# Last image's routing split seven blocks and one, and expert weights held in nine places and reloaded by halves

## Chip, core and metric

The kernel runs on one core of a Trainium2 chip. The metric is device time in microseconds (us) from launch to the last instruction, median of several executions. All arithmetic is fp32. The engines have separate in-order instruction streams: TensorE (PE, with PEld for its weight loads), VectorE (DVE), ScalarE (ACT), GpSimd (POOL) and SyncE (SP). In this kernel SP issues nearly all DMAs, ACT a few stores, POOL the gathers. A queue waits at its head: an instruction that waits holds back all behind it on that engine.

## The reference

Four images of 128 channels x 4096 positions pass through two layers, each adding to its input: a convolutional attention (softmax over 4096 x 4096 scores), and then a token layer that does a second attention and an expert feed-forward. The feed-forward is what the change is about:

```
logits = x @ gate_w.T + gate_b           # 4096 tokens x 64 experts, x layer-normalised
probs = softmax(logits, axis=1)          # over the tokens of the image
topv, topi = top 8 tokens of each expert
pooled[e] = sum_k topv[k,e] * x[topi[k,e]]
out[e] = gelu(pooled[e] @ weight1[e] + b1[e]) @ weight2[e] + b2[e]     # 128 -> 512 -> 128
y[topi[k,e]] += topv[k,e] * out[e]
```

So each image needs, per expert, its eight best tokens, the softmax sum, and the weighted sum of those tokens; one matrix product pair per expert; and a spread of the results over the tokens, done as a product with a matrix M that holds the probabilities of the chosen tokens and zeros elsewhere.

## The kernel before

The work is a series of stages, `stage(b, layer, ...)`, one per image `b` and attention layer; the last is `stage(3, 1)`. Each runs eight query blocks `n` of 512 tokens, and each block eight steps `g` of four key tiles. At every step one piece of the other work is emitted: `step_after` advances what follows a finished block (`finish_attn`), `beside` prepares the next stage. A fence that costs no instruction (`tc.no_sync_barrier`) keeps emitted work in its step; within the fences a planner orders each engine's instructions by when it computes that they are ready. `tc.keep_in_program_order` forbids it to move one instruction ahead.

`finish_attn` for block `n` combines the products (L626-636), divides and adds the residual (L645-654), normalises the tokens (`norm_tokens`, with the power on POOL, L181), stores them in DRAM in `tokens` (L614) for the later gather, turns them to channel order, and computes the gate logits into `M` (L696-701) and each block's eight largest per expert into `cand` (L704). Blocks other than the last of image 3 are turned with a DVE transpose and DMAs through DRAM (L321, L333, L683); the last one with PE transposes and ACT copies (`to_channels`, L356-357).

Routing of images 0 to 2 lies beside a later stage (`route`). Image 3 has none to lie beside. After its last block, `early_sums` takes exponential sums of seven blocks (L826) and `last_route` does the rest: `places` finds the eight places (maximum L729, index search over 4096 columns L731), `gather` fetches four token rows per partition by indirect DMA on POOL (L740), `replace` (L747) writes a copy of M without the eight best, `weigh` (L766-768) and a product with `twin` (L775) give the pooled vectors in `pooledT` (L776), and exponentials (L866) with DVE subtractions (L867) turn M into the spread matrix, whose discarded copy `z` is in a 2 MB buffer.

The experts go in 16 groups of four. A group's weights (first and second matrix, two halves of 1 MB) are one 2 MB load from a packed copy in DRAM (L947). Groups 0 and 1 are loaded during `stage(3, 1)`, 2 to 7 after it into buffers that attention leaves, group 8 into `z`, and 9 to 15 through a ring of four. Per group: `first_product` (L1013) and its copy (L1018), `hidden` (four PE transposes L1023, bias L1027, Gelu on ACT L1031), `second_product` (L1043). The loop emits the first product of group g, the hidden step of g-1 and the second product of g-2. After the loop come a range check (`watch`, from L1578), transposes of the results to expert order (L1061-1062), a reload of the first two images' M (2 MB, L1069) and of the inputs `x2` (eight of 1 MB, L1079), and per image pair eight products with M (L1092), each added by DVE (L1099); every two blocks are stored by two DMAs of 0.5 MB (L1102).

## Time and profile before

| what | value |
|---|---|
| median of 3 runs | 3320.46 us (3320.09 to 3320.47) |
| profiled execution: its own time / span of instructions | 3322.09 / 3320.4 us |
| PE busy | 3226.2 us, 97% |
| DVE, ACT, POOL busy | 2119.4, 1250.7, 413.3 us |
| last attention product ends | 3174.98 us from the span's start |
| first expert product starts | 3214.31 us |
| last expert product of the loop ends | about 3280.3 us |
| DMA, mean over the span | 68 GB/s |

Times in the views are us from the start of the span unless they are durations. In a timeline row come start, duration, engine, line, operation, tiles written and read, and the number of instructions joined in the row. The table by stage gives for each engine busy time and instruction count, then the clock that PE was granted as a share of full speed, the mean busy share of the 16 DMA engines and their rate.

### The profile page before, as it was taken

The page shows a single profiled execution, that of the slowest core. Times are in us where ns is not written, and L with a number is a line of the kernel's source. Part 1 is how long each engine was busy: PE and PEld are TensorE (multiplying, and loading weights), DVE is VectorE, ACT ScalarE, POOL GpSimd, SP SyncE. Part 2 cuts the span into 40 slices and gives each one's busy share as a digit, 9 for nine tenths or more (in the row PEclk, how much of TensorE's full clock was granted, in tenths as well). Part 3 has the DMA queues.
Part 4 walks back from the last instruction along what each step waited for, and adds up shares of the span by engine and source line. Part 5 has one row for each costly group of instructions (what it writes and reads, how often), then busy time and mean ns, then how long its engine had stood idle before and what let it go on. Part 6 is the DMA issues. An engine that isn't in the chain of part 4 may idle for free. (4 is left out here: it accounts for less than half of the span.)

```text
span 3320.4 us, 49374 instructions
## 1 busy us (share of the span) xinstructions
PE 3226.2 (97%) x19744; PEld 1603.4 (48%) x19744; DVE 2119.4 (64%) x4186; ACT 1250.7 (38%) x1429; POOL 413.3 (12%) x410
## 2 busy tenths in 40 slices
PE   8999999999999999999999999999999999999966
PEld 4444444445555544444555554444454454445433
DVE  6665577556675667755766566865775656665654
ACT  3333333333333344333333335333333333443330
POOL 0111113310000004230000003241000002100000
PEclk9999999999999999999999999999999999999977
DMA  3221244223232312301211112311221111021158
GB/s 87 51 54 26 67 107 123 76 77 85 79 85 72 81 32 60 70 23 33 52 42 23 36 36 64 80 42 28 68 51 33 30 30 39 23 80 30 33 227 368
DMA packets 367345, 224.36 MB, mean 68 GB/s; under 512 B 277632, under 2 KB 303232, under 8 KB 363776
## 3 DMA queue, kind: packets, MB, share of 16 engines
q1 hardware_dynamic: 361264, 209.59, 23.3%
q10 hardware_dynamic: 5328, 10.46, 0.8%
q8 instruction: 157, 2.57, 0.3%
q0 software_dynamic: 512, 1.05, 0.1%
q14 instruction: 84, 0.69, 0.1%
HBM read 160.27 MB, written 97.98 MB: 78 GB/s over the span
## 5 line engine op out<-in xcount | busy, mean ns | idle before, releaser
L550 ACT ACTIVATE pt<-ps 128x1024 f32<-128x1024 f32 x1024 | 1021.9, 1025 | 1536.0 <-PE ps L541 1464.3
L541 PE MATMUL ps<-q,t 128*64 128x512 f32 x4096 | 929.7, 593 | 0.0
L475 PE MATMUL av<-pt,asm 64*128 64x512 f32 x4096 | 922.2, 589 | 0.9 <-ACT sw L628 0.9
L565 DVE TENSOR_TENSOR sacc<-sacc,pt 128x1024 f32<-128x1024 f32 x448 | 586.4, 1309 | 291.4 <-ACT pt L550 266.7
L503 PE MATMUL av<-pt,tt 128*64 128x256 f32 x3072 | 637.5, 379 | 0.0
L475 PEld LDWEIGHTS av<-pt,asm 64*128 64x128 f32 x4096 | 395.8, 187 | 485.5 <-issue 470.0
L489 DVE TENSOR_TENSOR tt<-pt 128x512 f32<-128x512 f32 x512 | 356.8, 697 | 380.0 <-ACT pt L550 361.0
L541 PEld LDWEIGHTS ps<-q,t 128*64 128x64 f32 x4096 | 316.3, 137 | 469.7 <-issue 442.8
L503 PE MATMUL av<-tt,mixed 128*64 128x256 f32 x2048 | 526.6, 380 | 5.2 <-DVE tt L489 5.2
L541 PE MATMUL ps<-e,e 64*128 64x512 f32 x2048 | 491.5, 598 | 2.0 <-DMA e<-ye 2.0
L503 PEld LDWEIGHTS av<-pt,tt 128*64 128x64 f32 x3072 | 359.6, 137 | 261.5 <-issue 137.9
L503 PE MATMUL av<-tt,tt 128*64 128x256 f32 x1024 | 305.4, 380 | 0.0
L503 PE MATMUL av<-pt,mixed 128*64 128x256 f32 x1024 | 305.1, 380 | 0.0
L541 PEld LDWEIGHTS ps<-e,e 64*128 64x128 f32 x2048 | 193.3, 187 | 230.2 <-issue 226.2
L503 PEld LDWEIGHTS av<-tt,mixed 128*64 128x64 f32 x2048 | 280.7, 137 | 9.0 <-DVE tt L489 6.5
L181 POOL TENSOR_TENSOR l_y<-l_v,mhalf 128x4 f32<-128x4 f32 x64 | 64.8, 1013 | 1625.4 <-DVE l_v L180 1625.0
L491 DVE TENSOR_TENSOR tt<-pt 128x256 f32<-128x256 f32 x512 | 219.7, 429 | 16.4
L490 DVE TENSOR_TENSOR pt<-tt,pt 128x256 f32<-128x256 f32 x512 | 219.3, 429 | 16.1
L503 PEld LDWEIGHTS av<-pt,mixed 128*64 128x64 f32 x1024 | 140.3, 137 | 61.1 <-DVE pt L490 0.3
L503 PEld LDWEIGHTS av<-tt,tt 128*64 128x64 f32 x1024 | 140.3, 137 | 2.1 <-DVE tt L491 0.8
L584 POOL TENSOR_TENSOR all_sum<-all_sum,c 128x512 f32<-128x512 f32 x32 | 44.0, 1375 | 520.5 <-DVE c L583 520.5
L182 DVE TENSOR_TENSOR l_z<-l_y 128x4 f32<-128x4 f32 x64 | 11.7, 183 | 96.1 <-POOL l_y L181 94.9
(200 smaller groups left out, 1761.0 us busy)
## 6 DMA issues: line engine op xcount, KB each, us to landing
wp<-in_weight_dram SPq DMA_DIRECT2D x128, 256.0 KB
w<-wp SPq DMA_DIRECT2D x16, 2048.0 KB
xq<-in_x_dram SPq DMA_DIRECT2D x32, 256.0 KB
rb<-inv SPq DMA_DIRECT2D x32, 256.0 KB
xT<-xt SPq DMA_DIRECT2D x128, 64.0 KB
ak<-xT SPq DMA_DIRECT2D x32, 256.0 KB
t<-kt SPq DMA_DIRECT2D x128, 64.0 KB
t<-t SPq DMA_DIRECT2D x32, 256.0 KB
```

The source lines that it names most:

```text
L181: nc.gpsimd.tensor_tensor(y[:, :k], v[:, :k], mhalf[:, :k], op=ALU.pow)
L182: nc.vector.tensor_mul(z[:, :k], y[:, :k], y[:, :k])
L475: nc.tensor.matmul(avs[b, 0, n][:, r, :], lhsT=values[b, 0][rows, j, :], rhs=pt[rows, h, :], start=(j == 0), stop=(j == NJ - 1),)
L489: nc.vector.tensor_sub(tt[:, 0:2, :], p4[:, :, 1, :], p4[:, 0, :, :])
L490: nc.vector.tensor_add(p4[:, 0, 1, :], tt[:, 1, :], p4[:, 0, 0, :])
L491: nc.vector.tensor_sub(tt[:, 2, :], p4[:, 1, 0, :], p4[:, 0, 1, :])
L503: nc.tensor.matmul(av[bass.ts(half, HC), bank, slot, :], lhsT=lhsT, rhs=rhs, start=first, stop=final, skip_group_check=True,)
L541: nc.tensor.matmul(ps[part, h, :], lhsT=key[:, part], rhs=q[rows, :], start=True, stop=True,)
L550: nc.scalar.activation(pt, ps, AF.Exp, scale=scale)
L565: nc.vector.tensor_add(sums[b, n], sums[b, n], pt)
L584: nc.gpsimd.tensor_add(all_sum, all_sum, c1)
```

## The change

The last image's routing is split. Block 6 of image 3 is now turned like block 7, by PE. When its logits are there, `early_route`, emitted in the remaining steps of block 7, finds the eight best of the first seven blocks, gathers those rows and takes the exponential sums. After block 7, `last_route` merges these eight candidates with block 7's own eight. Early candidates that drop out get weight zero; the chosen tokens of block 7 are not fetched from DRAM but multiplied: their weights as a 64 x 512 matrix, transposed by PE, times the block's tokens in SBUF. Block 7's tokens are therefore not stored. The replacement over all of M (`last_scores`) comes after the expert loop's step 11 and its exponentials after the loop, with the subtractions on POOL.

The weights have nine places of 2 MB: 0 and 1 are the buffers of the last keys and values, filled by halves in the last block through a hook of `stage`; 2, 6 and 7 are loaded earlier in the stage, 3 to 5 after it, and 8 lies in the space that `finish_attn`'s buffers leave. Groups 9 to 15 go to places 0 to 6, first halves when the first product has used the old one, second halves when the second product has. The M reload goes to place 7, the inputs to 0 to 3. The range check moves to step 11 of the loop, the transposes to expert order to the end of each half of the loop, and the layout of w1's bias (`w1bT`) into the stage. The last block's copies and logits are split between ACT and DVE.

```diff
...
-        for name, side in (("blk", "left"), ("att", "right"), ("prep", "right"))
+        for name, side in (("blk", "right"), ("att", "right"), ("prep", "right"))
...
     def store_tokens(b, n, tb):
         rows = tokens[b][bass.ts(n, BLK), :].rearrange("(s p) c -> p s c", p=P)
-        q = nc.scalar if b == B - 1 and n == NB - 1 else nc.sync
-        q.dma_start(out=rows, in_=tb)
+        nc.sync.dma_start(out=rows, in_=tb)
...
-        if b == B - 1 and n == NB - 1:
-            c0 = av[:, 0, :]
+        direct, final = b == B - 1 and n >= NB - 2, b == B - 1 and n == NB - 1
+        if final:
+            c0, b1 = av[:, 0, :], av[:, 1, :]
         else:
             nc.scalar.copy(c0, av[:, 0, :])
-        nc.scalar.copy(c1, av[:, 1, :])
+            nc.scalar.copy(c1, av[:, 1, :])
+            b1 = c1
         nc.scalar.copy(sw[lo, :], av[hi, 1, :])
         nc.scalar.copy(sw[hi, :], av[lo, 1, :])
         one, two = slice(0, HB), slice(HB, BLK)
-        nc.vector.tensor_add(c1, c1, sw)
+        nc.vector.tensor_add(c1, b1, sw)
...
-        for k, (s0, ns) in enumerate(((0, 3), (3, 1))):
+        for k, (s0, ns) in enumerate(((2, 2), (0, 2)) if final else ((0, 3), (3, 1))):
...
-        if b == B - 1 and n == NB - 1:
+        if direct:
             norm_tokens(xT, tb, f"l2_{b}_{n}")
-            store_tokens(b, n, tb)
+            if not final:
+                store_tokens(b, n, tb)
             xp = block_tile("xp", f"xp{nm}")
             to_channels(xT, xp, f"x2_{b}_{n}")
             nc.scalar.dma_start(out=x2[b][:, bass.ts(n, BLK)], in_=xp)
             yield
-            to_channels(tb, tg, f"l2_{b}_{n}")
+            if final:
+                last_tokens.append(tb)
+                for h, copy in enumerate((nc.scalar.copy, nc.vector.tensor_copy)):
+                    pt = ms_tile(f"l2_{b}_{n}_{h}")[:, :HB]
+                    for s in range(SUB // 2):
+                        nc.tensor.transpose(
+                            pt[:, bass.ts(s, P)], tb[:, h * SUB // 2 + s, :], ident
+                        )
+                    copy(tg[:, bass.ts(h, HB)], pt)
+            else:
+                to_channels(tb, tg, f"l2_{b}_{n}")
...
+            if final and h == 1:
+                nc.vector.tensor_scalar(
+                    m[:, bass.ts(h, HB)], pg[part, :HB], gate_b[part, :], None, op0=ALU.add
+                )
+            else:
+                nc.scalar.activation(
+                    m[:, bass.ts(h, HB)], pg[part, :HB], AF.Identity, bias=gate_b[part, :]
+                )
         nc.vector.max(out=cand[b][hs, n, :], in_=m)
+        if b == B - 1 and n == NB - 2:
+            after.append(early_route(b))
...
-    def gather(b, at, got):
+    def gather(b, at, got, count=S):
...
-                out=got[:, bass.ts(k, C)], out_offset=None, in_=tokens[b],
+                out=got[:, bass.ts(k, C)], out_offset=None, in_=tokens[b][:count, :],
...
-    def early_sums(b):
+    early = {}
+    def early_route(b):
         hs = half_of(b)
+        m = M[b // 2][hs, : S - BLK]
         top, neg = small_tile("e_top", b, 8), small_tile("e_neg", b, 1)
...
+        at, tot = small_tile("r_at", b, 8, mybir.dt.uint32), small_tile("e_tot", b, NB)
+        nc.vector.max(out=top[hs, :], in_=cand[b][hs, : NB - 1].rearrange("p n k -> p (n k)"))
...
+        nc.vector.max_index(out=at[hs, :], in_max=top[hs, :], in_values=m)
+        yield
+        nc.vector.tensor_copy(cand[b][hs, NB - 2, :], top[hs, :])
+        got = block_tile("c0", f"got{b}")
+        gather(b, at, got, S - BLK)
+        junk = block_tile("xp", f"junk{b}")
         for n in range(NB - 1):
...
+            nc.scalar.activation(
+                junk[hs, :], m[:, bass.ts(n, BLK)], AF.Exp, bias=neg[hs, :],
+                accum_out=tot[hs, n : n + 1],
+            )
+            if n % 3 == 2:
+                yield
...
-        return top[hs, 0:1], tot[hs, NB - 1 : NB]
-    def last_route(b, early, late, dst):
+        early[b] = top[hs, 0:1], tot[hs, NB - 1 : NB], got
+    LOW, HIGH = -3.0e38, 3.0e38
+    def last_route(b, dst):
         hs = half_of(b)
...
+        early_max, early_tot, got = early.pop(b)
+        block = M[b // 2][hs, S - BLK :]
+        tokens_b = last_tokens.pop()
+        both = cand[b][hs, NB - 2 :, :].rearrange("p n k -> p (n k)")
+        top, neg = small_tile("r_top", b, 8), small_tile("r_neg", b, 1)
...
+        exps = block_tile("u", f"exps{b}")[hs, :]
+        z = block_tile("u", f"zl{b}")[hs, :]
+        nc.vector.max(out=top[hs, :], in_=both)
...
+        nc.scalar.activation(exps, block, AF.Exp, bias=neg[hs, :], accum_out=tot[hs, 1:2])
         nc.scalar.activation(scale[hs, :], early_max, AF.Exp, bias=neg[hs, :])
+        nc.scalar.activation(w8[hs, :], both[:, :8], AF.Exp, bias=neg[hs, :])
+        nc.vector.match_replace(
+            out=rest[hs, :], in_to_replace=top[hs, :], in_values=both, imm_value=LOW
+        )
...
+        )
+        nc.vector.match_replace(
+            out=z, in_to_replace=find[hs, :], in_values=block, imm_value=LOW
+        )
...
-        wgt = weights_of(b, top, neg, tot)
-        z = late.tile([P, S], F32, tag="z", name=f"z{b}", bufs=1)[hs, :]
+        inv = inv_tot[hs, b // 2 : b // 2 + 1]
+        nc.vector.reciprocal(inv, tot[hs, 0:1])
+        nc.scalar.activation(exps, exps, AF.Copy, scale=inv)
+        nc.vector.scalar_tensor_tensor(
+            w8[hs, :], in0=rest[hs, :8], scalar=LOW, in1=w8[hs, :], op0=ALU.is_le, op1=ALU.mult
+        )
...
+        nc.vector.scalar_tensor_tensor(
+            z, in0=z, scalar=LOW, in1=exps, op0=ALU.is_le, op1=ALU.mult
+        )
+        halves = block_tile("c1", f"halves{b}")[:, :C]
+        weigh(got, wgt, halves)
+        pw = ms_tile(f"pzT{b}")[:, : SUB * E]
+        for s in range(SUB):
+            nc.tensor.transpose(pw[:, bass.ts(s, E)], z[:, bass.ts(s, P)], ident[hs, hs])
+        wT = block_tile("xp", f"zT{b}")[:, : SUB * E]
+        nc.scalar.copy(wT, pw)
+        pq = ms_tile(f"pool{b}")
+        for s in range(SUB):
+            nc.tensor.matmul(
+                pq[:, :E], lhsT=tokens_b[:, s, :], rhs=wT[:, bass.ts(s, E)], start=(s == 0),
+                stop=False,
+            )
+        nc.tensor.matmul(pq[:, :E], lhsT=halves, rhs=twin, start=False, stop=True)
+        nc.vector.tensor_copy(dst[:, :, b], pq[:, :E])
+        return top, neg
+    def last_scores(b, top, neg):
+        hs = half_of(b)
+        m = M[b // 2][hs, :]
+        z = late_place[hs, :]
         tc.keep_in_program_order(replace(b, top, z))
         yield
-        halves = late.tile([P, H], F32, tag="hp", name=f"halves{b}", bufs=2)[:, :C]
-        weigh(got, wgt, halves)
-        pool_halves(b, halves, dst)
         for part in QUARTERS:
             for t in (z, m):
-                nc.scalar.activation(t[:, part], t[:, part], AF.Exp, bias=neg[hs, :])
-            nc.vector.tensor_sub(m[:, part], m[:, part], z[:, part])
+                tc.keep_in_program_order(
+                    nc.scalar.activation(t[:, part], t[:, part], AF.Exp, bias=neg[hs, :])
+                )
+            nc.gpsimd.tensor_sub(m[:, part], m[:, part], z[:, part])
+        yield
...
+            if hook:
+                hook(n, g)
...
-    W = {}
-    def weights(g, pool, tag):
-        W[g] = w = pool.tile([P, 2, EG * H], F32, tag=tag, name=f"w{g}")
-        nc.sync.dma_start(out=w, in_=packed[g])
+    W, places_of = {}, {}
+    def place(i, t):
...
+        places_of[i] = t.rearrange("p (h x) -> p h x", h=2)
+    def new_place(i, pool, tag):
+        place(i, pool.tile([P, 2 * EG * H], F32, tag=tag, name=f"w{i}"))
+    def load(g, i, h):
+        W[g] = places_of[i]
+        nc.sync.dma_start(out=W[g][:, h, :], in_=packed[g][:, h, :])
+    w1bT = const.tile([P, NHC, E], F32, tag="w1bT", name="w1bT")
     def first_weights():
+        w1b = block_tile("xq", "w1b", 4)[:E, :]
+        nc.sync.dma_start(out=w1b, in_=a["weight1"][:, D1 - 1, :])
         yield from idle(2)
-        weights(0, seq, "k")
-        yield from idle(4)
-        weights(1, seq, "v")
-        yield
+        new_place(6, seq, "k")
+        new_place(2, extra, "w")
+        for g in (6, 2):
+            for h in range(2):
+                load(g, g, h)
+        yield from idle(2)
+        pw = ms_tile("pw")
+        for c in range(NHC):
+            nc.tensor.transpose(
+                pw[:, bass.ts(c, E)], w1b.rearrange("e (p c) -> e c p", c=NHC)[:, c, :],
+                ident[:E, :E],
+            )
+        nc.scalar.copy(w1bT.rearrange("p c e -> p (c e)"), pw[:, : NHC * E])
+        yield from idle(2)
+        new_place(7, seq, "v")
+        for h in range(2):
+            load(7, 7, h)
+        yield
+    def last_weights(n, g):
+        if (n, g) == (0, 0):
+            place(0, keys[B - 1, 1])
+            place(1, values[B - 1, 1])
+        if n == NB - 1:
+            if g == NG // 2 - 1:
+                load(0, 0, 0)
+            if g == NG // 2:
+                load(1, 1, 0)
+            if g == NG - 1:
+                load(0, 0, 1)
...
+    extra = ctx.enter_context(tc.tile_pool(name="extra", bufs=1, reuse_waits="tile"))
     stage(3, 1, chain(done_after(route(2)), first_weights()), None,
-          ahead=mix_values(3), pace=(2, 1))
+          ahead=mix_values(3), pace=(2, 1), hook=last_weights)
     products()
     ends["att"].close()
-    ring = ctx.enter_context(tc.tile_pool(name="ring", bufs=4, side="right", reuse_waits="tile"))
-    w1b = seq.tile([E, H], F32, tag="mixed", name="w1b", bufs=1)
-    nc.sync.dma_start(out=w1b, in_=a["weight1"][:, D1 - 1, :])
-    for g in range(2, 6):
-        weights(g, ring, "w")
-    weights(6, seq, "v")
-    weights(7, seq, "k")
-    step_after()
-    early = early_sums(B - 1)
+    pooledT = seq.tile([P, E, PAD], F32, tag="mixed", name="pooledT", bufs=1)
+    nc.gpsimd.memset(pooledT, 0.0)
+    nc.gpsimd.tensor_copy(pooledT[:, :, 0 : B - 1], pooled[:, :, 0 : B - 1])
     while after:
         step_after()
+    ring = ctx.enter_context(tc.tile_pool(name="ring", bufs=3, reuse_waits="tile"))
+    load(1, 1, 1)
+    for g in range(3, 6):
+        new_place(g, ring, "w")
+        for h in range(2):
+            load(g, g, h)
+    last_top = last_route(B - 1, pooledT)
     ends["blk"].close()
-    late = ctx.enter_context(tc.tile_pool(name="late", bufs=1, reuse_waits="tile"))
...
-    weights(8, late, "z")
-    for g in range(9, E // EG):
-        weights(g, ring, "w")
+    late = ctx.enter_context(tc.tile_pool(name="late", bufs=1, side="right", reuse_waits="tile"))
+    late_place = late.tile([P, S], F32, tag="z", name="late_place")
+    place(8, late_place)
+    scores = last_scores(B - 1, *last_top)
+    for h in range(2):
+        load(8, 8, h)
     outT = late.tile([P, B, E], F32, tag="outT", name="outT")
-    osb = seq.tile([P, E // EG, O], F32, tag="mixed", name="osb", bufs=1)
+    osb = late.tile([P, E // EG, O], F32, tag="osb", name="osb")
...
+            for q in range(half * half_g // EG, (half + 1) * half_g // EG):
+                by_expert(q)
+    def by_expert(q):
...
-    watch(ms_tile("watch")[0:1, 0:1])
-    for q in range(E // EG // EG):
...
-    M[0] = seq.tile([P, S], F32, tag="k", name="M0b")
-    nc.sync.dma_start(out=M[0], in_=first_pair)
+        for half, now in ((0, g), (1, g - 2)):
+            if 0 <= now and now + 9 < E // EG:
+                load(now + 9, now, half)
+        if g == half_g + 3:
+            next(scores)
+            watch(ms_tile("watch")[0:1, 0:1])
+    next(scores)
+    M[0] = places_of[7].rearrange("p h x -> p (h x)")
+    tc.keep_in_program_order(nc.sync.dma_start(out=M[0], in_=first_pair))
     WIDE = 2 * BLK
     HS = S // 2
     ys = []
     for i in range(B // 2):
         for q in range(2):
-            pool, tag = ((seq, "k"), (seq, "v"), (seq, "v"), (late, "z"))[2 * i + q]
-            y = pool.tile([P, 2, HS], F32, tag=tag, name=f"y{i}_{q}")
-            ys.append(y)
+            ys.append(places_of[2 * i + q])
             for h in range(2):
-                nc.sync.dma_start(out=y[:, h, :], in_=x2[2 * i + h][:, bass.ts(q, HS)])
+                tc.keep_in_program_order(
+                    nc.sync.dma_start(out=ys[-1][:, h, :], in_=x2[2 * i + h][:, bass.ts(q, HS)])
+                )
...
```

## The prediction

> **What bounds the kernel now.** I read the page's slices first: PE is busy 90% or more everywhere but in the last two, so the change can only pay in the last 146 us; then the table by stage of that tail, in unequal steps.
>
> ```profile
> PE   8999999999999999999999999999999999999966
> ```
>
> ```profile
> 3174.00:3204.00 30.00, 6.55 (x42) 3.79 (x38) 18.43 (x46) 12.26 (x28) 1.01 (x1) 0.61 0.95 388
> 3204.00:3223.00 19.00, 9.35 (x60) 3.72 (x64) 9.30 (x14) 8.44 (x9) 6.03 (x6) 0.63 0.06 15
> 3223.00:3293.00 70.00, 50.53 (x682) 31.59 (x676) 27.02 (x53) 9.44 (x15) 0.00 (x0) 0.81 0.94 391
> 3293.00:3301.00 8.00, 7.14 (x28) 2.03 (x28) 7.46 (x7) 0.00 (x0) 0.00 (x0) 1.00 0.71 286
> 3301.00:3316.00 15.00, 8.59 (x32) 2.11 (x28) 10.24 (x9) 0.00 (x0) 0.00 (x0) 0.92 1.02 401
> ```
>
> Columns are stage and length, busy time of PE, PEld, DVE, ACT, POOL, PE clock, share and rate of DMA. The DMA engines are full (0.94 to 1.02) in three stages; they idle 19 us before the expert loop (0.06) and some 6 us where the result's products begin. In the loop PE works 50.5 of 70 us. So the tail is a stream of transfers with two holes. The chain of waits says what makes the first hole:
>
> ```profile
> 3187.61 17.54 DMA tk<-tb
> ...
> 3210.00 2.44 DMA got<-tk,r_rows
> ...
> 3214.31 3.64 PE ph L1013 x16
> ...
> 3281.57 0.59 DVE ok L1578
> ...
> 3284.22 3.62 PE pot L1061 x16
> ```
>
> Block 7's token store lands 17.54 us after its issue, since weight loads fill the queues; only then do the gathers go. They end at 3212.4, and the expert products start at 3214.31. After the loop, range check and transposes stand in the way of the result. The waits of SP's queue show why the weights do not fill the hole:
>
> ```profile
> SPq L947 <- DVE M L867: 27.8, 1, 27.8
> ```
>
> Group 8's load goes into z's buffer, free only after the first-step subtractions (L867), at 3223.0; groups 9 to 15 stand behind it. The last answer shows work that is moved: the index search (L731), the replacement (L747), and a DVE product (L491, normally 0.42) that meets a POOL subtraction.
>
> ```profile
> 2895.58 4.85 POOL L809 TENSOR_TENSOR M<-M,z 64x1024 f32<-64x1024 f32 x2 [19.97 <-ACT z L808]
> 2895.69 2.53 DVE L491 TENSOR_TENSOR tt<-pt 128x256 f32<-128x256 f32 x1
> ...
> 3192.06 4.42 DVE L731 FIND_INDEX8 r_at<-r_top,M 64x8 uint32<-64x4096 f32 x1
> ...
> 3197.69 4.41 DVE L747 MATCH_REPLACE8 z<-r_top,M 64x4096 f32<-64x4096 f32 x1
> ```
>
> **The change, part by part.** All times are of the profiled execution (span 3320.4, own time 3322.09); its span happens to lie at the median of the runs, 3320.46, so I subtract the difference in spans from the median.
>
> *Attention's end, 3174.98 before.* Block 6's eight PE transposes are new in a stage where PE never idles: four cost 0.68 in the loop at full clock, so 1.36. The four for w1bT move there too, 0.74 at half clock, so 0.37. `early_route` beside block 7 is bounded by its elder, image 2's routing: that block took 62.84 (the copies L626 stand at 2847.96 and 2910.80) against 53.81, so 9.0 at most, and 0 at least, because what block 6 loses (two DVE transposes of 0.70, its DMAs) held nothing up. Of the 9.0, PE waited 5.2 for DVE, as the waits in that stretch say:
>
> ```profile
> PE av L503 <- DVE tt L489: 5.2, 2, 3.9
> ```
>
> Ahead of those waits stood a replacement of 4.41, four exponentials of 1.15 and, on POOL, gathers before the power. The new piece has no replacement, seven exponentials of 0.86 spread over three steps, and an index search of 4.42 x 3584/4096 = 3.9; image 2's search alone left PE full until the replacement began. DVE idles 3.1 in each step of 6.4. I take 1.0, nearest to that search. Attention then ends at 3174.98 + 1.36 + 0.37 + 1.0 = 3177.7 (call it A). SP's new loads in block 7 wait for scores or products of steps 3, 4 and 7; behind them stand only other weight loads, since block 6's token store is issued at step 2 and block 7 stores none. POOL's four gathers (1.0 each), memset (1.82) and copy (0.34) end before block 7's power is asked for, some 9 us after A. ACT's store issue (0.34) lies in its idle time.
>
> *From A to the first expert product, 39.3 before (3174.98 to 3214.31).* Candidates of block 7 stood at 3191.62, 16.6 after. Off go one copy (0.6), the wait of the residual for early sums behind ACT (0.8) with the 2+2 split (0.4), and half of the last copy and bias by ACT (0.7): 14.1. Then follows the new merge: maximum and negation 0.4; exponential with read 0.9 and the scale 0.3 on ACT; sum and reciprocal 0.4; scaling 0.7; masking 0.7; `weigh` 1.3 beside or before it, of which I count 0.6; four transposes 0.8; copy 0.4; five products at half clock 0.33 each, 1.7; copy 0.3; with ten hand-overs of 0.05: 7.7. Small DVE steps (0.2 each) lie beside ACT. So 21.8: the product starts at 3199.5, 14.8 earlier. The gathered rows were asked for 20 us before, and the search, store and gather (4.4 + 17.5 + 7) are off the path. Bounds: 20.5 with `weigh` wholly hidden, 25 if DVE runs all of it in series.
>
> *The transfer stream.* 2 MB took 2.097/0.424 = 4.95 in the full stretch. After A come seven halves and the x2 store, 7.6 MB: 17.9, plus 2.0 from issue to first effect (a gather, the smallest transfer, lands 2.4 after issue), until A + 19.9. Before, 13 loads and a small one were left at that point, now 11.5 units of 2 MB: groups 6, 2, 7, 0 and half of 1 are there. Group 8 waits until `finish_attn`'s buffers are read for the last time, at about A + 21 (bounds 19 to 22); with 1.5 to restart, its data flow at 3200.2. Eight units of weights, M and four of x2: 13 x 4.95 = 64.3, until 3264.5. The result, 8.39 MB at 401 GB/s, 20.9: 3285.4. The last 1 MB (2.6) can't leave before the last addition; a hole of 0 to 2.6, I take 1.3. Before, the stores ended at 3316.5 (DMA share 0.12 of the last 4.4) and the span at 3320.4: 3.9 more. Sum: 3290.6, 29.8 below 3320.4, so 3290.7 from the median. Place by place nothing else holds this stream: first products of groups 0 to 6 end by A + 39 and second products by A + 45 (2.55 each, as at 3227 to 3238), while the stream asks for those places later.
>
> *PE beside it.* The first eight groups took 25.7 (3214.31 to 3240.0). The last half of weights lands at 3200.2 + 39.6 + 2 = 3241.8; the last second product (1.9), copy 1.22, eight transposes 1.8 and the way to the product (0.3 + 0.5 + 0.7): result products from 3248. They need 20 of DVE (16 x 1.23), the stores 21, so up to about 3258 their start costs nothing. This 10 us covers the replacement (4.4) and the range check (2.65) now inside the loop's DVE stream, which cost up to 7.1 without that cover. It also covers M: table load 1.28, eight exponentials of 1.13 and POOL's four subtractions of 2.45 after the last Gelu, some 14, while the second pair needs the first quarter 10 us after result products begin. POOL can block a DVE operation for 2 us, as L491's 2.53 shows, four times at most: 8, again inside.
>
> *A rule against the halves.* Loads of 1 MB replace loads of 2 MB, and the trace has 1 MB loads: the x2 reload, which fills these stretches.
>
> ```profile
> 3276.00:3280.00 4.00, 1.92 (x36) 1.57 (x36) 1.20 (x2) 0.63 (x1) 0.00 (x0) 0.92 1.00 412
> 3280.00:3284.00 4.00, 0.30 (x8) 0.00 (x0) 3.47 (x14) 0.00 (x0) 0.00 (x0) 0.50 1.02 424
> ```
>
> At 412 and 424 GB/s they are as fast as the 2 MB loads, so I charge nothing. The Trainium skill, "DMA: Bandwidth & Descriptors", section Bandwidth, gives 341 GB/s for a single 1 MB transfer against 425 for 16 MB, and asks for 1 MB only to reach three quarters of the peak. By that the 24.1 MB of weights after A would take 70.7 instead of 56.9, and the time would be 3304.5; its transfers run alone, these are queued back to back.
>
> **The rivals.** (1) *The loop's chain takes the place of the DMA.* From group 10 on PE ran po, ph, copy, transposes, bias, Gelu, po in series, 5.0 per group and 6.6 when the clock fell to 0.7, though the weights had landed. If the order stays so, the loop takes its 66 us again: 3199.5 + 66 = 3265.5, with replacement and check 3272.6; plus 4.5 to the products and 31.0 from there as before: 3301 to 3308. For it: nothing in the diff names the order. Against: the first half of group g+2 now comes before the second half of g, so that its first product can go ahead. (2) *Block 7 stalls* as image 2's routing did: 8 more, 3299. (3) *Slower: lock-step reloads.* SP is one queue; if a half stands in it whose place is freed late, all later ones, M and x2 wait. A group in lock-step costs issue to effect 2.0, transfer 4.95 and chain 6.6, 13.5 against 4.95, so 8.6 each; from the fourth of seven on it is slower (29.8/8.6 = 3.5), with five 3334. For it: before, group 8 held seven groups for 27.8 in just this way. Against: the places freed belong to groups 0 to 6, whose weights are there before the loop starts. (4) *The hole only moves:* group 8's buffer is freed late, or the merge runs in series with it by a wait that I do not see; 20 back, 3311.
>
> **How the numbers follow.** Likeliest (stream bound) 0.58, chain 0.19, stall 0.11, lock-step 0.07, moved hole 0.05. The likeliest has 3284 to 3297 of its own: stall 0 to 4, hole 0 to 2.6, group 8 two earlier or one later, rate 424 to 431. To leave no more than 2 in 10 out, the range goes to the chain's 3308 and so takes in the stall: 3284 to 3308. About 0.2% (6.6 us) is what counts as a difference. All cases but lock-step are faster, except the tail of the moved hole, so 0.91, 0.01 and 0.08.
>
> **What would show it.** First product 20 to 25 us after attention's end; no index search, gather or replacement between them; DMA share above 0.9 from there to the end but for about 2 us; result products starting at or before 3258 and y additions waiting for x2; group 15's second half landed near 3240. I am wrong if the last eight groups still take over 5 us each with their weights landed, if block 7 of image 3 takes over 57, or if an SP load in the loop waits several us for PE with the DMA engines idle.

## The result, and the profile after

The changed kernel takes 3298.83 us (median of 4 runs, 3294.15 to 3299.49) against 3320.28 for the kernel before, a ratio of 0.9933 with a 95% interval of 0.9915 to 0.995: 21.5 us faster where 29.8 were forecast, inside the range of 3284 to 3308 but above the likeliest case's own 3284 to 3297. Run again beside the first experiments, it took 3296.5 against 3321.0 (ratio 0.9925, 0.9911 to 0.9938). The profiled execution has a span of 3297.0 and an own time of 3298.76.

In the slices of the changed kernel's page, PE's last slice but one has 8 where it had 6; the rest of the row is as it was.

```profile
PE   8999999999999999999999999999999999999986
```

The table by stage of the same execution, cut at attention's end, the first expert product, the stall in the loop, its end, the first result product and the last store. Columns as before: stage and length, PE, PEld, DVE, ACT, POOL, PE clock, DMA share and rate.

```profile
3179.20:3202.53 23.33, 9.21 (x42) 6.20 (x43) 13.84 (x54) 6.13 (x12) 3.19 (x3) 0.56 0.91 354
3202.53:3236.20 33.67, 33.66 (x504) 19.70 (x504) 19.39 (x28) 6.93 (x11) 0.00 (x0) 0.95 1.00 402
3236.20:3242.10 5.90, 0.14 (x5) 0.16 (x7) 5.51 (x15) 0.63 (x1) 0.00 (x0) 0.81 1.01 417
3242.10:3262.19 20.09, 15.15 (x220) 8.58 (x219) 9.26 (x16) 8.60 (x10) 2.49 (x2) 0.84 1.01 420
3262.19:3293.00 30.81, 20.34 (x64) 5.61 (x64) 21.18 (x17) 3.59 (x4) 6.83 (x3) 0.78 0.91 346
3293.00:3297.00 4.00, 0.00 (x0) 0.00 (x0) 0.00 (x0) 0.00 (x0) 0.00 (x0) 0.50 0.11 41
```

The gap in front of the expert loop, 39.3 us before, is 23.3. The 19 us in which the DMA engines stood at 0.06 are gone: they are at 1.00 to 1.01 from the first expert product to the first result product. Three things in these rows were not forecast. PE is full in the second row (33.66 of 33.67 us), so the loop has no slack there. In the third row PE does nothing for 5.9 us. And the DMA share falls to 0.91 where the result is stored. The chain of waits names the links:

```profile
3202.53 3.49 PE ph L1127 x16
...
3234.42 4.42 DVE late_place L768
...
3242.14 3.58 PE ph L1127 x16
...
3262.19 3.81 PE px L1217 x8
3266.02 1.23 DVE t L1224
3267.72 4.18 DMA out_dram<-t
3271.97 9.32 DMA w<-x
3281.40 1.23 DVE w L1224
```

The replacement (L768) and the range check behind it on DVE end at 3241.8, and only then does PE go on with the expert products; the check's own little product stands in PE's queue ahead of them. Result products begin at 3262.19. Further down stands something odd: a result store, then a load of x2 that is issued only once that store has landed, at 3271.97. The waits of SP's queue say the same:

```profile
SPq L1041 <- DVE halves L789: 16.1, 1, 16.1
...
SPq L1203 <- DMA out_dram<-t: 13.8, 1, 13.8
```

The first line is group 8's load, which waits for the weighing as forecast (A + 20.2, where A is attention's end; 21 was taken). The second was in no view of before: the last 1 MB of x2 waits 13.8 us for a store that ACT issued. Its place had long been free. The compiled kernel's own list of instructions gives the waits of each: of the last x2 load on SP's queue, and of the second result store on ACT's.

```
L1203 DMACopy w3<-x2_3 [waits DMAHW3_49,PE_49]
L1227 DMACopy out_dram<-t3 [waits DMAHW7_49,DMAHW3_49]
```

A semaphore is a counter: a transfer adds to it when it has landed, and an instruction can wait until it stands high enough. Eight of them (DMAHW0 to DMAHW7) are handed round over the transfers of both queues, and both of these come to DMAHW3. A reading that fits is that SP waits until the store has counted on it. In steps of 4 us:

```profile
3236.00:3240.00 4.00, 0.19 (x8) 0.00 (x0) 3.97 (x5) 0.00 (x0) 0.00 (x0) 0.98 1.02 416
3240.00:3244.00 4.00, 2.04 (x14) 0.79 (x18) 1.89 (x12) 0.63 (x1) 0.00 (x0) 0.50 1.05 440
...
3264.00:3268.00 4.00, 4.00 (x14) 1.15 (x10) 3.24 (x4) 1.78 (x2) 4.00 (x3) 0.60 0.32 125
3268.00:3272.00 4.00, 3.39 (x15) 0.90 (x12) 3.90 (x4) 0.00 (x0) 1.02 (x1) 1.00 0.97 380
3272.00:3276.00 4.00, 3.81 (x14) 0.90 (x12) 3.77 (x4) 0.00 (x0) 0.00 (x0) 1.00 1.01 284
3276.00:3280.00 4.00, 3.56 (x15) 1.07 (x16) 3.65 (x4) 0.00 (x0) 0.00 (x0) 1.00 0.94 335
```

PE's 5.9 us of idling cost more than themselves, since the granted clock then is 0.50 for 4 us. From 3264 to 3268 the DMA engines stand at 0.32, 2.7 us lost; and after that, while the late load runs beside the stores, they are busy and move only 284 and 335 GB/s.

So two theories went to the chip: that the check holds PE, and that the shared semaphore holds the last load. Their rival is the forecast's own view, that the loop has 10 us of slack and the transfers end when they end. The other runs undo one part of the change each, to see which part the gain came from.

### The profile page after: what moved, and what is told of

It reads as the page before. It is cut to its first block, busy times and chain, and to the rows that moved or that the text cites. A ratio compares the mean times of both kernels' runs of the same rounds, so it can differ in the third digit from the quotient of the medians.

```text
span 3297.0 us, 49453 instructions
## 1 busy us (share of the span) xinstructions
PE 3227.0 (98%) x19764; PEld 1602.7 (49%) x19764; DVE 2123.0 (64%) x4192; ACT 1253.4 (38%) x1432; POOL 424.4 (13%) x414
## 4 chain that ended last, share of the span: by engine, by line
PE 96%; DVE 2%; DMA 1%; issue 0%; POOL 0%; ACT 0%; SPq 0%; ACTq 0%; DVEq 0%; POOLq 0%
PE ps L542 40%; PE av L476 27%; PE av L504 23%; PE pe L272 1%; PE pa L291 1%; PE pq L445 1%; PE pv L647 1%; PE ph L1127 1%; PE pg L710 0%; PE po L1157 0%; PE pd L590 0%; PE pht L1137 0%; DMA w<-x 0%; DVE tt L490 0%; DMA first_x<-in_x_dram 0%
```

## Experiments

### The changed kernel again

No edit. It gives the next three runs a neighbour on their own chip.

> The changed kernel as it is, run beside the next three on the same chip, so that they are compared with it and not only with the kernel before. Its runs so far lay between 3294.2 and 3299.5 us. Both theories: 3298.8, within 3294 to 3299.5; result products (px) begin at 3262.2, the last x2 load is issued at 3272.0, the DMA engines are at a third of their share in the four microseconds from 3264.

Measured: 3296.5 (3296.03 to 3296.94), span 3294.9. Attention ended at 3177.1, not 3179.2; from there the steps have the same length as in the first profile (first product after 23.4, result products after another 59.6). So 2 us of the first profiled execution lie ahead of attention's end, and are a spread between executions. The last x2 load was issued at 3269.6, and the lost transfer time is spread differently (0.61 and 0.53 in the two windows from 3260), with about the same loss in all. The runs below are compared with this one; the later ones ran on two other chips, where the kernel before took 3321.11 and 3321.84 in place of 3321.0.

### The range check after the stores

```diff
             next(scores)
-            watch(ms_tile("watch")[0:1, 0:1])
...
+    watch(ms_tile("watch")[0:1, 0:1])
```

(The added line stands behind the loop over the result's blocks.)

> The range check is taken out of step 11 of the expert loop and made after the last result addition; the replacement stays in step 11. Theory A (PE was itself the bound of the loop, and the check, whose product stands in PE's queue, held it for its own length on top of the replacement): PE is held some 3.3 us instead of 5.9 at step 11, result products begin 2.6 us earlier, at about 3259.6, the first stores go out 2.6 earlier, the last x2 load behind them too, and the end comes 2.6 earlier: 3296.2. Theory B (the loop has slack there, as the prediction said, and only the transfers count): result products move or not, the end stays, 3298.8 give or take 0.5.

Measured: 3293.84 (3292.75 to 3295.72), 2.7 earlier, as theory A had it (2.6). The loop gained more than the check's length: result products begin 55.7 us after the first expert product, where they began after 59.6. The windows of this run show why:

```profile
3232.00:3236.00 4.00, 2.90 (x48) 1.59 (x44) 3.97 (x2) 0.00 (x0) 0.00 (x0) 1.00 1.02 422
3236.00:3240.00 4.00, 1.82 (x24) 1.51 (x28) 2.54 (x4) 1.26 (x2) 0.00 (x0) 1.00 1.01 418
3240.00:3244.00 4.00, 3.19 (x76) 2.16 (x68) 1.38 (x2) 0.63 (x1) 0.00 (x0) 1.00 0.99 420
```

PE's longest waits there are 2.43 and 0.85 us in place of 5.76, and the granted clock stays at 1.00 in these windows. In the changed kernel the 5.76 were followed by half clock, at which sixteen products took 3.58 us (eight take 1.04 at full clock).

The last x2 load still waited 13.0 us for a store, which only came earlier. So this run says that PE's hold is on the path; it does not speak for or against the semaphore.

### The last two x2 loads from POOL's queue

```diff
-    next(scores)
...
             for h in range(2):
+                queue = nc.gpsimd if 2 * i + q >= 3 else nc.sync
                 tc.keep_in_program_order(
-                    nc.sync.dma_start(out=ys[-1][:, h, :], in_=x2[2 * i + h][:, bass.ts(q, HS)])
+                    queue.dma_start(out=ys[-1][:, h, :], in_=x2[2 * i + h][:, bass.ts(q, HS)])
                 )
+    next(scores)
```

> The last two x2 loads (place 3) are issued by POOL's queue instead of SP's, ahead of POOL's four subtractions; nothing else. Theory A (the last load stood behind a result store because both use the same DMA semaphore): it is issued as soon as group 12's second product has read its place, before 3260 instead of 3272.0, the hole of some 2.7 us from 3264 to 3268 is filled, and the end comes 2.5 to 3 earlier, 3296 (the additions, 16 of 1.23 from 3266, then set the pace as much as the stores). Theory B (the place is freed late, or the DMA engines have nothing to do with the end): issue still after 3268 or the end unchanged, 3298.8. A cost of its own: if POOL waits at that load for long, its subtractions come late and the result products with them, up to 5 us slower.

Measured: 3291.83 (3291.74 to 3293.39), 4.7 earlier, more than theory A's 2.5 to 3. The timeline of this run has the two loads:

```profile
3242.37 0.63 POOL L1201 DMA_DIRECT2D w<-x  x1 [55.97 <-PE ph L1127]
...
3248.34 0.54 POOL L1201 DMA_DIRECT2D w<-x  x1 [5.34 <-PE po L1157]
```

The last one waits for group 12's second product (L1157), which frees its place, and goes out at 3248.3 in place of 3269.6. So the place was not what held it. POOL's subtractions were not late: result products begin at 3259.9, in the run before at 3260.1. The windows from 3260 on stand at 1.02, 0.84 and 1.02, and from 3272 to 3276 at 407 GB/s, where the two profiles of the changed kernel have 284 and 270. That is the part that the expectation missed: besides the hole, the low rate went.

### Both

The two edits together.

> Both: range check after the stores, and the last two x2 loads from POOL's queue. If both holds are real and in series, the gains add: result products from 3259.6, no hole, transfers end 5.3 earlier, 3293.5. A bound from the transfers alone: the stream is full until 3264, then 1 MB of x2 (2.6) and 8.39 MB of result at 401 GB/s (20.9) and 3.9 to the end give a span of 3291.4, 5.6 under the 3297.0 of the changed kernel. If only one of the two counts, 3296.

Measured: 3291.93 (3290.38 to 3294.45), no better than the load alone by its time: a gain of 4.6, where 5.3 were expected for the sum (3293.5 was counted from 3298.8). Two things show in the trace. PE waited 2.43 and 0.85 us as in the run with the check moved, but here the granted clock fell to 0.50 from 3240 to 3244 all the same, and result products begin 58.4 us after the first expert product in place of 55.7: what a short stall costs by the clock differed between these two executions. The Trainium skill, "TensorE: Matmul & The Clock Gate", Part 1, says that the clock halves after an idle window of about 3.4 us, and that the windows run freely; 5.76 agrees, and of the two runs with 2.43 and 0.85 one kept the clock and one didn't. And with the load free even these 1.2 us of the result products hardly show in the end, which the next run tests.

The profiles can be compared without the spread ahead of attention's end. From there to the end of the span the changed kernel takes 117.8 us, with the check moved 114.1 (in that run the first expert product, too, came 0.9 sooner), with the load freed 114.0, with both 113.2. The gains of 3.7 and 3.8 come to 4.6 together and not to 7.5: the two holds lie in series, since PE's hold delays the store for which the load waits.

### The replacement in four pieces as well

```diff
-        tc.keep_in_program_order(replace(b, top, z))
-        yield
+        for part in QUARTERS:
+            tc.keep_in_program_order(nc.vector.match_replace(
+                out=z[:, part], in_to_replace=top[hs, :], in_values=m[:, part], imm_value=-3.0e38
+            ))
+            yield
...
-        if g == half_g + 3:
+        if half_g <= g < half_g + 4:
             next(scores)
```

> On top of the run with both edits (check after the stores, last two x2 loads from POOL), the replacement is cut into four pieces of 1024 columns, one in each of steps 8 to 11 of the loop. A piece takes out the eight values only where they stand in it, and this is the same as the whole only where no value stands twice. Theory A (with the hole filled, the transfers are the bound from the start of the loop to the end): result products begin up to 3 us earlier, the end moves by at most 0.5: 3291.5. Theory B (PE's hold is still on the path, by the clock that falls while PE idles and by the additions' pace): the end comes 2 to 3 earlier, 3289.

Measured: 3289.46 (3288.11 to 3292.2), on another chip than the run with both; the ranges overlap (3290.38 to 3294.45), so the times do not settle whether it is faster. The first result store goes out 2.7 us earlier, as the two timelines say, first of the run with both:

```profile
3263.16 4.39 ACTq L1225 DMA_DIRECT2D out_dram<-t  x4
```

and with the pieces:

```profile
3260.51 5.21 ACTq L1228 DMA_DIRECT2D out_dram<-t  x4
```

The stores end where they ended: in the window from 3284 to 3288 the DMA share is 0.46 with both and 0.52 with the pieces, and from attention's end to the end of the span both executions take 113.2 us, though result products begin 3.4 earlier with the pieces. So in these two executions the transfers are the bound, and theory A holds. For the other runs it is open: the profiled one, at 3292.2, was the slowest of its four, and the other three (3288.1 to 3289.8) lie near theory B's 3289. Neither the forecast (slack in the loop) nor its opposite is wholly right: while the last load waits for a store, the end hangs on PE; with the load free it hangs on the transfers, as far as the traces show.

### The last load's semaphore alone

POOL's queue differs from SP's in more than its semaphores. This run leaves all loads on SP and makes one store of two, so that the semaphores fall differently: the last x2 load now shares its own with an earlier x2 load.

```diff
             if k % 2 == 1:
-                for h in range(2):
-                    nc.scalar.dma_start(
-                        out=out[2 * i + h][:, bass.ts(n // 2, WIDE)],
-                        in_=y[:, h, bass.ts(k // 2, WIDE)],
-                    )
+                nc.scalar.dma_start(
+                    out=out[2 * i : 2 * i + 2][:, :, bass.ts(n // 2, WIDE)].rearrange("h p c -> p h c"),
+                    in_=y[:, :, bass.ts(k // 2, WIDE)],
+                )
```

> The changed kernel, with the two result stores of 512 KB that follow each second addition made into one of 1 MB; x2 loads all stay on SP's queue. The stores now take other DMA semaphores, and the last x2 load shares its own with an earlier x2 load and not with a store. Theory A (the shared semaphore held the last load): it is issued from SP before 3256, no hole from 3264 to 3268, the end 3 to 4.5 earlier than the changed kernel run beside the first experiments (3296.5), as when POOL issued it: 3292 to 3293.5. Theory B (SP's queue itself was the trouble, and POOL's the cure): issue after 3266, end 3295.5 to 3297.

Measured: 3291.66 (3290.32 to 3292.93), 4.8 earlier than the changed kernel, though on another chip (where the kernel before took 3321.84, 0.8 more). SP issues the four loads between these bounds, the last at 3254.7. It waits 4.6 us for an earlier x2 load, the one with which it now shares a semaphore, and not for a store, though its place was free from 3248.0, when group 12's second product ended:

```profile
3239.80 15.24 SPq L1203 DMA_DIRECT2D w<-x  x4
```

```profile
SPq L1203 <- DMA tt<-x: 4.6, 1, 4.6
```

```profile
3260.00:3264.00 4.00, 4.00 (x10) 1.50 (x12) 3.56 (x3) 3.40 (x4) 4.00 (x2) 0.50 1.02 420
3264.00:3268.00 4.00, 3.64 (x14) 0.90 (x12) 3.63 (x4) 0.00 (x0) 2.63 (x2) 0.91 0.87 341
3268.00:3272.00 4.00, 3.61 (x16) 0.90 (x12) 3.90 (x4) 0.00 (x0) 0.00 (x0) 1.00 1.01 401
3272.00:3276.00 4.00, 3.78 (x16) 0.90 (x12) 3.75 (x4) 0.00 (x0) 0.00 (x0) 1.00 1.03 407
```

Result products begin at 3259.8 and the check is where it was, so this gain is the load's. Theory A stands: it was the shared semaphore, not SP's queue, and the load still follows its semaphore here, to another transfer. One thing is confounded: the stores are 1 MB here. But the run with POOL's loads kept 512 KB stores and reached 407 and 408 GB/s too.

### Semaphore, check and pieces, all on SP

The three edits (check after the stores, pieces, one store for two).

> The changed kernel with the range check after the stores, the replacement in four pieces in steps 8 to 11, and one store of 1 MB in place of two; x2 loads all on SP's queue. The pieces are the same as the whole only where no value stands twice. Theory A (shared semaphore and the hold of the loop are the two causes): 3289.5, within 1.5, as with the loads from POOL. Theory B (POOL's queue was needed): 3292 to 3294.

Measured: 3292.84 (3289.37 to 3293.37), span of the profiled execution 3290.1. The median lies in theory B's range (3292 to 3294) and outside theory A's, which only the fastest of the five runs reaches; on the same chip one store alone took 3291.66, so check and pieces add nothing that shows here. The trace shows the stores ending in the same window as with POOL's loads (share 0.59 from 3284, then 0.04). So theory B's reason does not follow from its number: POOL's queue is not needed, as one store alone showed too. Which of these versions is the fastest is open: their ratios to the kernel before, 0.9904 (0.9889 to 0.9919) for the pieces with POOL's loads, 0.9908 (0.9893 to 0.9923) for one store alone, 0.991 (0.9897 to 0.9924) here, overlap. Each beats the changed kernel's 3296.5 on its own runs. The one with a single edit is the one to keep.

### Undone: the tokens multiplied and not gathered

The last block's tokens are stored by ACT's queue, and the old search, gather and weighing over all eight blocks take the place of the merge; the early routing keeps its exponentials only.

```diff
+            q = nc.scalar if final else nc.sync
+            q.dma_start(
+                out=tokens[b][bass.ts(n, BLK), :].rearrange("(s p) c -> p s c", p=P), in_=tb
+            )
...
+        top, neg, at = places(b)
+        got = block_tile("c0", f"got{b}")
+        gather(b, at, got)
...
+        weigh(got, wgt, halves)
+        pool_halves(b, halves, dst)
```

> The changed kernel, with the last block's tokens stored and gathered as in the kernel before (store by ACT's queue, search over all eight blocks, gather, weighing, one product with the doubled identity), in place of the merge and the product with the block's own tokens; early exponentials, places, loads ahead, halves and the replacement in the loop stay. Theory A (store and gather behind the full queues are what kept the loop from starting): first expert product 13 to 17 us later, at about 3215 with attention's end at 3177.2, the group 8 load with it, and the end as much later as PE and the stream both stand behind it: 3311, between 3307 and 3314. Theory B (the loads made ahead and in halves carry most of the gain): product as late, but the loop then finds its weights there and makes half of it good, end 3300 to 3305.

Measured: 3304.17 (3303.61 to 3306.46), 7.7 slower than the changed kernel, in theory B's range, but not by its way: the loop made hardly any of the delay good. The timeline of this run:

```profile
3187.74 0.38 ACTq L667 DMA_DIRECT2D tk<-tb  x1
...
3192.02 4.42 DVE L754 FIND_INDEX8 r_at<-r_top,M 64x8 uint32<-64x4096 f32 x1
...
3200.74 1.05 POOL L763 DMA_INDIRECT got<-tk,r_rows  x1 [15.03 <-issue]
...
3208.92 1.94 PE L1082 MATMUL ph<-t,pooledT 128*32 128x512 f32 x8 [0.56 <-DVE pooledT L799]
```

The store takes 11.9 us to the moment at which POOL and ACT go on (3199.6), not 17.5 as before. More of the weights have been loaded during attention and fewer stand ahead of it: the DMA engines are full until 3196 (share 1.02) and at 0.42 in the next 4 us, while in the kernel before they are full until 3200 and at 0.81 in the next 4 us. The first product starts 8.4 later than in the changed kernel, not 13 to 17, and the end 7.7 later. So search, store and gather were worth about 8 here. Of the gap's shrinking from 39.3 to 23.3 another 7 us stay in this run; 5.6 of them are the store's shorter way.

### Undone: the early routing

```diff
-        if b == B - 1 and n == NB - 2:
-            after.append(early_route(b))
...
+    run(early_route(B - 1))
```

> The changed kernel, with the early routing (search, four gathers, seven exponentials) put behind block 7's last step instead of beside block 7. Theory A (the routing beside block 7 is worth what the prediction counted): the search (3.9), the row copies (0.4), four gathers' issue (4.0) and landing (2.4 to 10 while the weight loads fill the engines) now stand between block 7's scores and the weighing, so that the first expert product starts 5 to 13 us later, and as PE bounds the loop the end comes as much later: 3306, between 3301 and 3311. Theory B (the merge of the last block is the longer chain, the early routing would have hidden anyway): first product less than 2 us later, end 3298 to 3300.

Measured: 3298.17 (3297.51 to 3299.69), 1.7 slower: theory B. (The profiled execution, the slowest of the five, takes 3.1 longer than the changed kernel from attention's end.) The edit did not do what it says, though. The timeline shows the search in the last microseconds of attention, before block 7's steps although it is written behind them:

```profile
3174.21 3.89 DVE L845 FIND_INDEX8 r_at<-e_top,M 64x8 uint32<-64x3584 f32 x1
...
3197.05 0.29 DVE L785 TENSOR_SCALAR halves<-got,r_wgt 128x128 f32<-128x128 f32 x1
```

The planner may move what depends on blocks 0 to 6 alone, and DVE waits there for attention's end: 4.6 us in the changed kernel. Counted from attention's end, the weighing and the first product came 2.1 later. So most of the early routing fits into holes of DVE, ACT and POOL that would be there anyway; what it would cost wholly in series was not measured. From the first copy of block 6 to attention's end block 7 took 50.9 us both with the routing beside it and with the search at its end: the stall that the forecast put at 1.0 does not show.

### Undone: the loads during the last block

```diff
-        if n == NB - 1:
-            if g == NG // 2 - 1:
-                load(0, 0, 0)
-            if g == NG // 2:
-                load(1, 1, 0)
-            if g == NG - 1:
-                load(0, 0, 1)
...
-    load(1, 1, 1)
+    for g, h in ((0, 0), (1, 0), (0, 1), (1, 1)):
+        load(g, g, h)
```

> The changed kernel, without the three loads of 1 MB into the last image's keys and values during its last block; they are issued after attention, ahead of the others. Theory A (the stream of transfers sets the end): 3.1 MB more after attention are 7.4 us at 425 GB/s, less the hole of about 1 us in front of group 8's load and the 2.7 us of the later hole: 3.7 later, 3301.5. Theory B (PE sets the end through the result products): no weights come late for PE, result products begin where they began, the end moves by less than 1: 3298.

Measured: 3299.55 (3297.29 to 3299.87), 3.0 slower; theory A's size (3.7), by a way that it did not name. Result products begin 3.6 later. Windows of this run:

```profile
3228.00:3232.00 4.00, 3.19 (x28) 1.73 (x28) 1.69 (x5) 0.63 (x1) 0.00 (x0) 1.00 1.01 414
...
3264.00:3268.00 4.00, 4.00 (x10) 1.41 (x12) 3.56 (x3) 3.31 (x4) 4.00 (x2) 0.50 0.02 8
```

PE is no longer full before the replacement (3.19 of 4 us, 4.00 in the changed kernel). No wait of PE in the loop is for a load, though: what it waits for, 0.81 us in this window, is the copy of a first product, since its instructions stand in another order than in the changed kernel. So what shows is the order that the planner made for later loads, and not weights that came late. The time then shows up as a longer hole at 3264, where the last load stands behind its store: the loop sets the stores, and the stores set the last load.

### Undone: halves reloaded apart

```diff
-        for half, now in ((0, g), (1, g - 2)):
+        for half, now in ((0, g - 2), (1, g - 2)):
```

> The changed kernel, with the first half of each reload (w1) issued not after the first product but after the second, together with the other half: two steps of 2.55 us later. Theory A (the reloads stand in a queue that is full anyway: the last of them is issued 16 us before its data flow): nothing moves, 3297 to 3299, DMA share stays at 1.0 from the loop's start on. Theory B (reloading in halves is what keeps the stream full): a gap of about 5 us in the DMA share after the loop's first steps, and the end 3 to 5 later, 3302.

Measured: 3307.18 (3303.54 to 3308.09), 10.7 slower, the dearest of the four, and more than twice what theory B had. Waits of SP's queue and windows of this run:

```profile
SPq L1041 <- PE po L1157: 12.1, 6, 6.3
```

```profile
3208.00:3212.00 4.00, 4.00 (x80) 2.96 (x83) 2.07 (x3) 0.63 (x1) 0.00 (x0) 1.00 0.19 39
...
3268.00:3272.00 4.00, 1.67 (x7) 0.87 (x5) 2.69 (x6) 4.00 (x5) 4.00 (x3) 0.50 0.03 12
3272.00:3276.00 4.00, 3.89 (x10) 1.63 (x12) 3.56 (x4) 1.39 (x2) 4.00 (x2) 0.50 0.01 2
```

SP stands 6.3 us at the second half of place 0, with the first halves of places 1 and 2 behind it, whose places are free. 3.2 us of the stream are lost at 3208. The queue that I had thought always full is full only because the halves go out as they come free.

The larger part is another. The second products of the last four groups begin at 3247.9, 3252.5, 3258.7 and 3263.7, 15.8 us from first to last, where the changed kernel takes 6.9. PE does not wait for weights there: none of its waits in the loop is for a load, and the last weights have landed by 3246.9, when SP's next load, which waits for them, goes out. It waits for its own chain:

```profile
3252.48 1.48 PE L1157 MATMUL po<-w,hT 128*32 128x128 f32 x32 [1.51 <-ACT hT L1145]
3253.71 1.95 PE L1127 MATMUL ph<-w,pooledT 128*32 128x512 f32 x8
3256.46 0.75 PE L1137 MATMUL pht<-ident,hp 128*128 128x128 f32 x4 [0.79 <-DVE hp L1132]
3258.72 1.08 PE L1157 MATMUL po<-w,hT 128*32 128x128 f32 x32 [1.51 <-ACT hT L1145]
```

First product, copy, transposes, Gelu and second product of one group run one after the other before the next group's first product. In the changed kernel a first product stands ahead of an earlier group's second product. So this is the chain of the prediction's first rival, and it comes back when the first halves no longer run ahead. The result products begin 10.5 later after attention's end, 8.9 of it from these four groups, and with the last load behind its store nearly 8 us of transfers are lost from 3268.

## Why the prediction was right, and where not

Measured in the two profiles of the changed kernel, against the prediction's own terms:

| term | forecast | first profile | second |
|---|---|---|---|
| attention's end, A | 3177.7 | 3179.2 | 3177.1 |
| A to first expert product | 21.8 | 23.3 | 23.4 |
| group 8's load after A | 21 | 20.2 | 20.2 |
| result products begin | 3248, limit 3258 | 3262.2 | 3260.1 |
| lost after the loop | 1.3 | 5.2 | 5.6 |
| span | 3290.6 | 3297.0 | 3294.9 |

"Lost after the loop" is the sum of 4 x (1 - rate / 415) over the windows of 4 us from 3260 to 3280, since the loads before them run at some 415 GB/s: in the first profile 2.8 + 0.3 + 1.3 + 0.8. With POOL's loads it is 1.0, with one store for two also 1.0.

**Attention's end** was right. Block 7 took 50.9 us from the first copy of block 6, before 49.4, so that the transposes cost about 1.5 where 1.36 was put; the stall of 1.0 does not show; the 2 us between the profiles lie ahead of block 7. (One reading at the prediction's start is off: of the 40 slices the first, too, is under 90%, with its 8.)

**From A to the first product** was 1.5 short: the weighing runs half in series with the rest on DVE, the choice between 20.5 and 25 that was named. The direction and the cause held: no search, gather or replacement stands in between, and with the gather put back the first product is 8.4 later.

**"At 412 and 424 GB/s they are as fast as the 2 MB loads, so I charge nothing"** was right. The halves ran at 412 to 426 GB/s from 3212 to 3236, not at the 341 that the Trainium skill ("DMA: Bandwidth & Descriptors", Bandwidth) gives for 1 MB; its table times single transfers, issued by GpSimd. What the sum lacked was the worth of their order, 10.7 us, which stood in the prediction only as the reason against the first rival.

**The stream up to the result** was right to about 2 us: 3264.5 was forecast for all weights, M and x2. In the first profile 0.5 MB moved in the 4 us after 3264, and the last 1 MB was not yet issued; at 415 GB/s these 1.55 MB are 3.7 us, which makes 3267.7, 1.7 later than forecast once A's 1.5 is taken off.

**"This 10 us covers the replacement (4.4) and the range check (2.65)" is the step that failed.** It compared the start of the result products with the stream and took the loop for a follower of its weights. In the first ten groups PE was itself the bound, 2.55 us per group without a gap; the prediction's own 2.55 for sixteen groups would have made 40.8 us, until 3240.3 against 3241.8 for the last weights, so there were no 7 us to cover. Whatever stops PE moves the result products: replacement and check stopped it for 5.9 us, and half clock added to that. They began 4.2 and 2.1 us after the limit of 3258 that the prediction itself had set. In the time this step counts only through the load of the next paragraph: moving the check gains 2.7 with the load held, and nothing that shows with the load free (3291.93 against 3291.83).

**"A hole of 0 to 2.6, I take 1.3" was mis-sized**, and for a reason that no term had: the hole isn't left by the last addition but by an x2 load that waits for a store. 3.9 to 4.3 us of the difference are here. With the load freed the spans are 3290.1 to 3291.1, at the forecast's 3290.6. From attention's end the forecast has 112.9 us; the kernel takes 114.0 with the load freed and 113.2 with the check moved too. The stream forecast is thus what the kernel reaches when these holds are taken away, not what it reached: that 3298.8 lies in the range is owed to the range's width for the rivals, not to the hole that was foreseen.

**The rivals.** The chain (3301 to 3308) did not come: the second products of the last four groups lie 6.9 us from first to last. The reason given against it held, since the run with both halves at one moment brings the chain back. The stall did not come. Lock-step did not come either; that same run shows it in small, 3.2 us of transfers lost behind one load whose place is freed late. The moved hole did not come. "An SP load in the loop waits several us" was named as a sign of error; it happened after the loop, for a store and not for PE.

Where the gain came from, part by part: undone alone, the halves cost 10.7, the gather 7.7, the loads ahead 3.0 and the early routing 1.7, against the changed kernel on the first chip, where the whole gain was 24.5; they ran on two other chips, where the kernel before took 0.1 and 0.8 more. They act on one another, so their sum of 23.1 is no proof of an account.

## What to carry to other kernels

Before work is called covered by slack, ask which engine is full in that stage: PE stopped here for 5.76 us for a product of 0.19 us in its queue whose operand was late, and went on at half clock (0.50 for 4 us). A stream of loads was here only as continuous as the order in its queue and the semaphores that its transfers share with others: look for a load that waits for a store, and change the number or the order of transfers until it shares with one that is long done. Splitting a reload so that each part goes out when its own half is free was worth 10.7 us, most of it because PE could then run a later group's first product ahead of an earlier group's second; one 2 MB reload per place was not run. When an undone part costs time, look first whether the engine waits for the data or only stands in another order.

## What the runs showed of the hardware

- Loads and stores at the same time move less: the engines' share was 1.01 and 0.94 at 284 and 335 GB/s while the last 1 MB of x2 ran beside the stores, and 407 to 408 GB/s for stores of the same size with that load out of the way. That 1 MB took 9.3 us to land; at the 415 GB/s of the loads before it, 1 MB is 2.5 us.
- A store's time to land went with what was issued ahead of it: 17.5 us before, 11.9 with more of the weights loaded earlier, in both runs until the DMA engines had emptied.
- A load whose place was free waited for another transfer on the same semaphore: 13.8 us for a store in the changed kernel, 4.6 us for an earlier load with one store for two, and not at all for a store when POOL issued it.
- The same kernel reached the end of attention 2.0 us apart in two executions of some 3180, at an unchanged length of each later step.
